# Transposing conv2's outputs: 28 of 64 graphs moved from TensorE to 32x32 blocks on VectorE

## The chip, the cores and the metric

The kernel runs on one core of a Trainium2 chip, in float32 throughout. A core has TensorE (PE in the profile; its weight loads are PEld), VectorE (DVE), ScalarE (ACT), GpSimd (POOL) and SyncE (SP), which work side by side and wait for each other by semaphores. Each takes its own instructions in a fixed order. DMAs are issued from SP, ACT and POOL and share 16 DMA engines. The metric is the device time of one launch in microseconds, as the median of several runs.

## The reference, cut to what matters

There are 64 graphs of 256 nodes with 256 features. Layer 0 is a graph convolution with a residual and a layernorm. Layer 1 takes its output x1 through two branches and a GRU cell:

```
xc     = transpose(x1)                              # features by nodes
h      = relu(bn1(conv1(xc)))                       # kernel size 1
h      = bn2(conv2(h))                              # 17 taps along the nodes
x_conv = transpose(relu(h + xc))
A      = exp(-dist(s, s)) * adj,  s = x1 @ w_se.T + b_se
x_nmp  = A @ relu(x1 @ w_msg.T + b_msg)
r, z, n from x_in = [x_conv, x_nmp] and x1          # GRU cell, weights w_ih, w_hh
out    = layernorm(x1 + (1 - z) * n + z * x1)
```

The change concerns one step: conv2's output plus x1, relu, in the layout that the gate matmuls read.

## The kernel before

**Groups.** The 64 graphs go in four groups of Q = 16. For each graph `layer0` and `layer1` run its two layers up to conv1 and x_nmp. conv2 is computed for a whole group at once by transforms: the group's conv1 outputs are transformed (`p_dft`), multiplied in frequency (`products`, `p_k`), and transformed back on VectorE (`real_transform`, `complex_begin`, `complex_end`). `output` stores the results, nodes by features, to the DRAM tensor `xc_d` of the group (L717). x1 is stored in `x1_d` by layer 0 (L410), and the transposed x1 together with x_nmp in `xn_d` (L509).

**Gates.** `gates(q, part)` runs the GRU cell of graphs of group q. The first EARLY = 4 graphs of groups 0, 1 and 2 run beside the layers of the next group: their pieces are interleaved with `layer0` and `layer1`. Graphs 4 to 15 of those groups run beside the next group's products and inverse transform, at a pace that `paced` sets. The last group has nothing beside it: its 16 gates run alone at the end.

**One gate.** `inputs` is a tile of 128 partitions by 6 by 256: slices 0 and 1 hold x1 transposed, 2 and 3 x_nmp, and 4 and 5 conv2's part (`xcT`). The steps are:

- `load_conv(g)` loads `xc_d` of the graph into the tile `xc_g` (L754, from SP), nodes on the partitions; `load_gate(g)` loads `x1_g` (L758) and slices 0 to 3 of `inputs` (L760).
- `residual(g)` adds x1 to `xc_g` in memory, by an adding DMA issued from POOL (L765).
- `transposed(g)` transposes `xc_g` by four TensorE instructions against the identity into the PSUM bank `p_xcT` (L776). ScalarE reads it, adds the bn2 bias, applies relu and writes `xcT` (L778).
- `input_sums(g)` forms four sums of 128x384 on POOL (L787 to L792, tile `sums`).
- `gru(g)` does seven blocks of three matmuls for r and z (`p_rz`, L808), with the sums as some of the operands, then two times six for n (`p_n`, L845). VectorE adds biases and combines (`first` L821, `trz`, `gn` L850 to L854, L868 to L870), ScalarE does the tanh, and the layernorm's inverse root is a power on POOL (`ln_rs`, L314).

`gru(g)` also prepares its successor: it calls `load_gate(g + 1)`, `residual(g + 1)`, `transposed(g + 1)`, `input_sums(g + 1)` and `load_conv(g + 2)`. `inputs`, `x1_g` and `xc_g` have two buffers each, `sums` one.

**Order.** A scheduler orders each engine's instructions when the kernel is built, by when it expects operands and free buffers; the source's order is a priority, not the outcome. `tc.issue_after(op)` keeps what is written inside it behind `op` on op's engine.

Of the kernel before, what the change touches and what calls it, by code (L numbers as in the profile page):

```python
# [9 lines left out]
F32 = mybir.dt.float32  # L10
AF = mybir.ActivationFunctionType
ALU = mybir.AluOpType
AX = mybir.AxisListType

P = 128
# [11 lines left out]
def kernel(  # L27
# [27 lines left out]
    nc = tc.nc  # L55
    B, N, D = x.shape
# [4 lines left out]
    DCH = D // P  # L61


    FL, NT = 48, 32
    GT = N // NT
    Q = P // GT
    NQ = B // Q
    assert N == 256 and D == 256 and B % Q == 0 and TAPS == FL - NT + 1 and FL == 3 * NT // 2
# [22 lines left out]


    xin, ain = {}, {}

    def load(g):
        if g >= B:
# [51 lines left out]
    bn2_bias = const.tile([P, DCH], F32)  # L148
# [51 lines left out]
    def tables(pool):  # L200
# [24 lines left out]
        with tc.issue_after(DIAGONAL[0]):  # L225
# [6 lines left out]
            for n0, n1 in ((0, 1), (1, 2), (2, 3), (3, 7), (7, NF)):  # L232
                nc.vector.tensor_scalar(
                    w_row[:, :, 1, n0:n1], fwd_row[:, :TAPS, IM[n0] : IM[n0] + n1 - n0], -1.0, None, op0=ALU.mult
                )
        for j in range(GT // 2 + 2):

# [91 lines left out]
    xc_d = [dram.tile([Q, N, D], F32, name=f"xc_d{q}") for q in range(NQ)]  # L329
# [92 lines left out]
    def layer1(g, place):  # L422
# [39 lines left out]

        mid = GT // 2
        if TILES[0] is not V:
# [284 lines left out]

    GATE, CONV, SUMS = {}, {}, {}  # L750

    def load_conv(g):
        CONV[g] = gate.tile([P, NCH, D], F32, name="xc_g")
        nc.sync.dma_start(CONV[g], xc_d[g // Q][g % Q].rearrange("(c p) d -> p c d", p=P))  # L754

    def load_gate(g):
        x1 = gate.tile([P, NCH, D], F32, name="x1_g")
# [2 lines left out]
        nc.sync.dma_start(inputs[:, : 2 * DCH], xn_d[g])  # L760
        GATE[g] = x1, inputs

    def residual(g):

        nc.gpsimd.dma_start(  # L765
            CONV[g], x1_d[g // Q][g % Q].rearrange("(c p) d -> p c d", p=P), accum_op=ALU.add
        )

    def transposed(g):

        xc = CONV.pop(g)
        xcT = GATE[g][1][:, 2 * DCH :]
        p = bank("p_xcT").rearrange("p (k n) -> p k n", k=DCH)
        for k in range(DCH):
            for c in range(NCH):
                nc.tensor.transpose(p[:, k, c * P : (c + 1) * P], xc[:, c, k * P : (k + 1) * P], ident)  # L776
        for k in range(DCH):
            nc.scalar.activation(xcT[:, k], p[:, k], AF.Relu, bias=bn2_bias[:, k : k + 1])  # L778
# [15 lines left out]
    def gru(g):  # L794

        following = g % Q + 1 < Q
        (x1, inputs), S = GATE.pop(g), SUMS.pop(g)
        trz = gate.tile([P, 4, D], F32, name="trz", bufs=1)  # L800
        nn = gate.tile([P, NCH, D], F32, name="nn", bufs=1)
        if following:
            load_gate(g + 1)
        A11, A12, A21, A22 = halves(inputs)

        def block(p, j, a, b):
            for k in range(HALF):
                nc.tensor.matmul(  # L808
                    p[:, j * D : (j + 1) * D], a[:, k], wrz[:, b, k], start=k == 0, stop=k == HALF - 1
                )  # L810

        p15, p26 = accbank("p_rz"), accbank("p_rz")
        block(p15, 0, A11, B11)
        block(p26, 0, A12, B21)
        block(p15, 1, S[:, 0], T1)
        block(p26, 1, S[:, 1], T2)
        yield
        if following:
            residual(g + 1)
        first = gate.tile([P, 2, D], F32, name="first", tag="gn")  # L820
        mark(nc.vector.tensor_add(first, half(p15), brz_t), 1)  # L821
        nc.vector.tensor_add(trz[:, 0:2], first[:, 0:1].to_broadcast([P, 2, D]), half(p26))
        p7, p34 = accbank("p_rz"), accbank("p_rz")
        block(p7, 0, S[:, 2], T3)
        block(p34, 0, S[:, 3], B22)
        block(p34, 1, A22, T4)
        nc.vector.tensor_add(trz[:, 3], trz[:, 1], p7[:, :D])
        mark(nc.vector.tensor_add(trz[:, 1:3], trz[:, 1:4:2], half(p34)), 1)

        nc.scalar.activation(trz[:, 0:4:2], trz[:, 0:4:2], AF.Tanh, scale=0.5)  # L830
        nc.vector.tensor_add(trz[:, 1:4:2], trz[:, 1:4:2], first[:, 1:2].to_broadcast([P, 2, D]))
        nc.scalar.activation(trz[:, 1:4:2], trz[:, 1:4:2], AF.Tanh, scale=0.5)
        if following:
            transposed(g + 1)
        yield
        for c in range(NCH):
            terms = [(inputs[:, k, c * P : (c + 1) * P], wn[:, k]) for k in range(3 * DCH)]
            if c == 0 and following:
                input_sums(g + 1)
            if c == 1 and g % Q + 2 < Q:  # L840
                load_conv(g + 2)
            p = accbank("p_n")
            for o, part in ((1, terms[:DCH]), (0, terms[DCH:])):
                for j, (lhsT, w) in enumerate(part):
                    nc.tensor.matmul(  # L845
                        p[:, o * D : (o + 1) * D], lhsT, w, start=j == 0, stop=j == len(part) - 1
                    )

            gn = gate.tile([P, 2, D], F32, name="gn")
            mark(nc.vector.tensor_add(gn, p.rearrange("p (i d) -> p i d", i=2), bn_t), 1)  # L850
            nc.vector.scalar_tensor_tensor(
                gn[:, 1, :], trz[:, 2 * c], 1.0, gn[:, 1, :], op0=ALU.add, op1=ALU.mult
            )
            nc.vector.scalar_tensor_tensor(  # L854
                gn[:, 0, :], gn[:, 1, :], 0.5, gn[:, 0, :], op0=ALU.mult, op1=ALU.add
            )
            nc.scalar.activation(nn[:, c, :], gn[:, 0, :], AF.Tanh)  # L857


            if g == B - 1:  # L860
                part = slice(c, c + 1)
            elif c == NCH - 1:
                part = slice(0, NCH)
            else:
                yield
                continue
            y, t, n = x1[:, part], trz[:, 1:4:2][:, part], nn[:, part]
            mark(nc.vector.scalar_tensor_tensor(y, t, 3.0, y, op0=ALU.add, op1=ALU.mult), 1)  # L868
            nc.vector.scalar_tensor_tensor(n, t, 1.0, n, op0=ALU.subtract, op1=ALU.mult)
            nc.vector.tensor_sub(y, y, n)  # L870
            layernorm(y, nc.scalar, 4 * LN_EPS)
            nc.scalar.dma_start(out[g].rearrange("(c p) d -> p c d", p=P)[:, part], y)
            yield
# [26 lines left out]
    def run(stage):  # L900
        for _ in stage:
            pass
# [72 lines left out]
        nc.vector.tensor_copy(bn_t[:, 0, :], bih_t[:, 2 * D :])  # L975
        nc.vector.tensor_copy(bn_t[:, 1, :], bhh_t[:, 2 * D :])
    ustream = ctx.enter_context(tc.tile_pool(name="ustream", bufs=6))
    EARLY = 4

    def open_ahead(graphs):  # L980

# [4 lines left out]
    def gates(q, part):  # L986

        for i in part:
            if i == 0:
                load_conv(q * Q)  # L990
                load_gate(q * Q)
                yield
                load_conv(q * Q + 1)
                residual(q * Q)
                yield
                transposed(q * Q)
                yield
                input_sums(q * Q)
                yield
            yield from gru(q * Q + i)  # L1000
# [18 lines left out]
    for q in range(NQ):  # L1019
        first = (q + 1) * Q  # L1020
        more = q + 1 < NQ
        end = chain(complex_end(q), copies(V2) if more else iter(()))
        if more:
            if q:
                others = [take(late, 3 if i % 3 == 0 else 2) for i in range(AHEAD)]
            else:
                others = [nothing() for _ in range(AHEAD)]
                ALONE.update(range(first, first + AHEAD))
            TILES[0] = V2
            begin = graphs(first, range(AHEAD), others)  # L1030
        sums(0)
        real = real_transform()
        for step in range(STEPS):
            if step < 4:
                run(products(step))
            else:
                run(merge(products(step), take(real, 1)))
                run(complex_begin(step))
            if q:
                run(take(late, (0, 1, 1, 1, 1, 1, 2, 1, 2, 1, 2, 1)[step] if more else step % 2))  # L1040
            else:
                run(take(begin, 3))
        run(real)
        if not q:
            run(paced(begin, end, RATES[q]))
        elif more:
            run(paced(chain(merge(take(late, 20), take(begin, 6), 3), begin), end, RATES[q]))
        else:
            run(paced(late, end, RATES[q]))
            run(end)  # L1050
        if more:
            run(late)
            run(end)
            if q == 0:
                scope.close()
                gate = ctx.enter_context(tc.tile_pool(name="gate", bufs=2))
            early = gates(q, range(EARLY))
            others = [take(early, 5 if q == 0 else 2) for _ in range(Q)]
            run(graphs(first, range(AHEAD, Q), others))
            run(early)  # L1060
            if q == 0:
                scope, AHEAD, V2 = open_ahead(6)
                ctx.enter_context(scope)
            late = gates(q, range(EARLY, Q))
        else:
            run(gates(q, range(Q)))


# [51 lines left out]
```

## Time and profile before

| | |
|---|---|
| median of three runs | 2167.7 us (2166.14 to 2169.88) |
| profiled execution | 2162.39 us |
| its span, first to last instruction | 2160.6 us |
| mean granted TensorE clock | 0.993 |
| busy: PE, DVE, ACT, POOL | 2058.4, 1547.2, 834.7, 665.5 us |
| DMA queues of SP, ACT, POOL: share of 16 engines | 30.0%, 8.7%, 8.5% |
| transposes of `xc_g` on PE | 256, four to a graph |
| adding DMAs | 64, issue 1.23 us, 4.8 us to landing (medians) |

All views come from one profiled execution, which is a little shorter than the runs that are timed. A row of a group gives line, engine, operation, the tiles written and read, how many, busy time and mean duration; the idle time before it is named with what ended it. A float32 matmul of 128x256 appears as two records on PE, so "x42" stands for 21 matmuls; a transpose appears as one. A PE duration includes the pipeline's length; back to back, instructions start closer together than they last.

### The profile page before, as it was taken

How to read it: one execution, taken by the hardware profiler on the slowest of the kernel's cores; microseconds unless marked ns; L12 is line 12 of the kernel's file. 1: busy time of each engine (PE TensorE's matmuls, PEld its weight loads, DVE VectorE, ACT ScalarE, POOL GpSimd, SP SyncE). 2: the span in 40 equal slices, each digit the busy share in tenths (PEclk: the TensorE clock that was granted, in tenths of full speed). 3: DMA queues.
4: the chain of work that ended last, by engine and by line, in shares of the span. 5: the costliest groups of instructions: out<-in, count | busy, mean ns of one | idle time of the engine just before them, and what ended most of it. 6: DMA issues, size and time to landing. Idle time of an engine off the chain costs nothing.

```text
span 2160.6 us, 29043 instructions
## 1 busy us (share of the span) xinstructions
PE 2058.4 (95%) x9805; PEld 1745.5 (81%) x9805; DVE 1547.2 (72%) x3691; ACT 834.7 (39%) x1857; POOL 665.5 (31%) x640
## 2 busy tenths in 40 slices
PE   7999999887999999899999999999999998999998
PEld 5888788776788888788888888778888887788887
DVE  5555577775568788775556988876556889977776
ACT  4665643456331123455443122446543122222222
POOL 2444310122431244223222133323231124444442
PEclk9999999999999999999999999999999999999999
DMA  4766666434347644243336654325334834444441
GB/s 122 236 193 199 194 197 209 144 123 153 87 123 228 195 110 135 98 132 113 108 94 189 201 165 112 118 99 153 92 97 134 249 113 120 126 123 103 113 107 54
DMA packets 251182, 305.65 MB, mean 141 GB/s; under 512 B 18174, under 2 KB 229714, under 8 KB 251034
## 3 DMA queue, kind: packets, MB, share of 16 engines
q1 hardware_dynamic: 183530, 200.46, 30.0%
q10 hardware_dynamic: 44480, 67.39, 8.7%
q0 software_dynamic: 23024, 35.95, 8.5%
q8 instruction: 78, 1.28, 0.2%
q14 instruction: 70, 0.57, 0.1%
HBM read 200.62 MB, written 103.06 MB: 141 GB/s over the span
## 4 chain that ended last, share of the span: by engine, by line
PE 45%; DVE 13%; issue 8%; POOL 6%; ACT 4%; DMA 1%; ACTq 0%; POOLq 0%; DVEq 0%
PE p_rz L808 17%; PE p_n L845 8%; PE p_k L530 7%; PE p_out L400 2%; PE p_nmp L504 2%; PE p_hT L390 2%; POOL ln_rs L314 1%; PE p_dft L471 1%; PE p_conv L434 1%; POOL xc_g L765 1%; POOL sums L788 1%; POOL sums L787 1%; PE p_msg L455 1%; PE p_dist L495 1%; ACT inputs L778 1%
## 5 line engine op out<-in xcount | busy, mean ns | idle before, releaser
L845 PE MATMUL p_n<-wn,inputs 128*128 128x256 f32 x1536 | 350.0, 381 | 14.8 <-DVE first L821 14.7
L808 PE MATMUL p_rz<-wrz,sums 128*128 128x256 f32 x1536 | 350.9, 381 | 3.3 <-POOL sums L787 2.4
L845 PEld LDWEIGHTS p_n<-wn,inputs 128*128 128x128 f32 x1536 | 285.8, 190 | 59.7 <-DVE first L821 17.9
L808 PEld LDWEIGHTS p_rz<-wrz,sums 128*128 128x128 f32 x1536 | 290.8, 191 | 48.1 <-issue 5.6
L808 PE MATMUL p_rz<-wrz,inputs 128*128 128x256 f32 x1152 | 271.9, 379 | 0.2
L314 POOL TENSOR_TENSOR ln_rs<-ln_rs,neg_half 128x2 f32<-128x2 f32 x129 | 100.5, 779 | 519.3 <-DVE ln_rs L313 448.0
L808 PEld LDWEIGHTS p_rz<-wrz,inputs 128*128 128x128 f32 x1152 | 217.5, 190 | 30.7 <-issue 1.0
L857 ACT ACTIVATE nn<-gn 128x256 f32<-128x256 f32 x128 | 53.2, 416 | 329.8 <-DVE gn L854 329.5
L530 PE MATMUL p_k<-u,VM 128*128 128x256 f32 x736 | 174.5, 380 | 1.6 <-DVE VM L573 0.9
L787 POOL TENSOR_TENSOR sums<-inputs 128x384 f32<-128x384 f32 x64 | 71.1, 1112 | 332.6 <-ACT inputs L778 299.8
L360 POOL TENSOR_TENSOR dis<-deg,neg_half 128x2 f32<-128x2 f32 x64 | 46.0, 718 | 401.6 <-DVE deg L358 389.6
L324 ACT ACTIVATE x_g<-x_g,ln_mr,ln_rs 128x256 f32<-128x256 f32 x128 | 70.0, 593 | 245.9 <-DVE ln_mr L322 245.9
L530 PEld LDWEIGHTS p_k<-u,VM 128*128 128x128 f32 x736 | 138.3, 190 | 22.5 <-DMA u<-ud 2.0
L471 PE MATMUL p_dft<-fwd,h 128*128 128x240 f32 x512 | 119.8, 378 | 27.8 <-ACT h L438 26.7
L390 PE MATMUL p_hT<-adjT,x 128*128 128x256 f32 x512 | 127.9, 392 | 14.4 <-DVE adjT L372 7.7
L471 PEld LDWEIGHTS p_dft<-fwd,h 128*128 128x128 f32 x512 | 95.4, 192 | 48.4 <-ACT h L438 41.6
L434 PE MATMUL p_conv<-wc,xn 128*128 128x259 f32 x512 | 125.8, 388 | 4.9 <-ACT xn L420 4.9
L383 POOL TENSOR_TENSOR x_t<-x_t,b_t 128x512 f32<-128x512 f32 x64 | 86.5, 1352 | 140.6 <-ACT x L382 88.6
L497 DVE TENSOR_TENSOR aT<-aT,adjT 128x512 f32<-128x512 f32 x64 | 44.3, 692 | 113.5 <-ACT aT L496 113.5
L400 PE MATMUL p_out<-w,hT 128*128 128x256 f32 x512 | 123.1, 383 | 1.4 <-ACT hT L395 0.7
L455 PE MATMUL p_msg<-wmsg,xn 128*128 128x256 f32 x512 | 121.5, 380 | 0.0
L504 PE MATMUL p_nmp<-aT,msg 128*128 128x256 f32 x512 | 121.1, 379 | 0.2 <-DVE aT L497 0.2
(154 smaller groups left out, 3898.6 us busy)
## 6 DMA issues: line engine op xcount, KB each, us to landing
u<-ud SPq DMA_DIRECT2D x284, 256.0 KB
xn_d<-xn ACTq DMA_DIRECT2D x64, 512.0 KB
inputs<-xn_d SPq DMA_DIRECT2D x64, 512.0 KB
ud<-u_set POOLq DMA_DIRECT2D x39, 480.0 KB, 6.0
adj_t<-in_adj_dram SPq DMA_DIRECT2D x64, 256.0 KB
x_t<-in_x_dram SPq DMA_DIRECT2D x64, 256.0 KB
x_d<-x ACTq DMA_DIRECT2D x64, 256.0 KB
xc_d<-VM SPq DMA_DIRECT2D x64, 256.0 KB
```

The lines of the kernel that those rows point to most:

```text
L314: nc.gpsimd.tensor_tensor(rs[:, : len(chunks)], rs[:, : len(chunks)], neg_half[:, : len(chunks)], op=ALU.pow)
L383: nc.gpsimd.tensor_tensor(x_t, x_t, b0_t.unsqueeze(1).to_broadcast([P, NCH, D]), op=ALU.add)
L390: nc.tensor.matmul(p[:, k, :], x1[:, mc, k * P : (k + 1) * P], adjT[:, mc, 1 - mc : 3 - mc, :].rearrange("p n q -> p (n q)"), start=mc == ...
L400: nc.tensor.matmul(p[:, c, :], hT[:, k, c * P : (c + 1) * P], w0[:, k, :], start=k == 0, stop=k == DCH - 1)
L434: nc.tensor.matmul(p, x1T[:, k, c * P : (c + 1) * P], wc1[:, k, :], start=k == 0, stop=k == DCH - 1)
L455: nc.tensor.matmul(p[:, c, :], x1T[:, k, c * P : (c + 1) * P], wmsg[:, k, :], start=k == 0, stop=k == DCH - 1)
L471: nc.tensor.matmul(p[:, t0 * FL : t1 * FL], h[:, c, k * P : (k + 1) * P], fwd[:, first : first + t1 - t0, :].rearrange("p t f -> p (t f)") ...
L504: nc.tensor.matmul(p[:, k, :], msg[:, mc, k * P : (k + 1) * P], aT[:, mc].rearrange("p n q -> p (n q)"), start=mc == 0, stop=mc == NCH - 1,)
L530: nc.tensor.matmul(p[:, j * D : (j + 1) * D], v[:, k, :], u[:, k, :], start=k == 0, stop=k == DCH - 1)
L787: nc.gpsimd.tensor_tensor(S[:, 0], A21, A22, op=ALU.add)
L808: nc.tensor.matmul(p[:, j * D : (j + 1) * D], a[:, k], wrz[:, b, k], start=k == 0, stop=k == HALF - 1)
L845: nc.tensor.matmul(p[:, o * D : (o + 1) * D], lhsT, w, start=j == 0, stop=j == len(part) - 1)
```

## The change

For 28 graphs (the first four of every group, and all of the last group) the transpose goes to VectorE, which transposes each 32x32 block within its 32 partitions. The blocks themselves are put in place by the load: `load_conv` issues four DMAs, one for each 32 features of a 128-feature half, and each moves pieces of 32 floats (128 bytes) so that after the blockwise transpose the tile is the full transpose. x1 is no longer added by the adding DMA. It is added after the transpose by POOL, from the x1 slices of `inputs`, and ScalarE's relu then reads and writes `xcT` in place. `behind` puts the VectorE instructions that are written after a transpose behind it on that engine. The other 36 graphs go as before.

```diff
+    RB = 32
+    NB = P // RB
...
+    order = ExitStack()
+
+    def behind(op):
+        order.close()
+        order.enter_context(tc.issue_after(op.ins))
...
+    EARLY = 4
+
+    def in_blocks(g):
+        return g % Q < EARLY or g >= B - Q
+
     def load_conv(g):
+        y = xc_d[g // Q][g % Q]
+        if in_blocks(g):
+            CONV[g] = gate.tile([P, DCH, N // RB, RB], F32, name="xc_blocks", tag="xc_g")
+            for b in range(NB):
+                nc.sync.dma_start(
+                    CONV[g][b * RB : (b + 1) * RB],
+                    y.rearrange("(s r) (k b j) -> b r k s j", r=RB, k=DCH, j=RB)[b],
+                )
+            return
         CONV[g] = gate.tile([P, NCH, D], F32, name="xc_g")
-        nc.sync.dma_start(CONV[g], xc_d[g // Q][g % Q].rearrange("(c p) d -> p c d", p=P))
+        nc.sync.dma_start(CONV[g], y.rearrange("(c p) d -> p c d", p=P))
...
+    def sent(g):
+        if not in_blocks(g):
+            residual(g)
...
     def transposed(g):
+        inputs = GATE[g][1]
+        xcT = inputs[:, 2 * DCH :]
+        if in_blocks(g):
+            behind(nc.vector.transpose(xcT.rearrange("p k (s r) -> p k s r", r=RB), CONV.pop(g)))
+            nc.gpsimd.tensor_tensor(xcT, xcT, inputs[:, :DCH], op=ALU.add)
+            for k in range(DCH):
+                nc.scalar.activation(xcT[:, k], xcT[:, k], AF.Relu, bias=bn2_bias[:, k : k + 1])
+            return
         xc = CONV.pop(g)
-        xcT = GATE[g][1][:, 2 * DCH :]
...
-            residual(g + 1)
+            sent(g + 1)
...
-                residual(q * Q)
+                sent(q * Q)
```

More of the change, by code (lines that the diff above doesn't have):

```diff
@@ L977 @@
     ustream = ctx.enter_context(tc.tile_pool(name="ustream", bufs=6))
-    EARLY = 4
     def open_ahead(graphs):
@@ L1066 @@
             run(gates(q, range(Q)))
+    order.close()
 _OUT = ((64, 256, 256), "float32")
```

## The prediction

> **What bounds the kernel now.** I read the busy shares first, then the stages, then the chain of waits inside one period, then the tile that the change touches.
>
> ```profile
> PE 2058.4 (95%) x9805; PEld 1745.5 (81%) x9805; DVE 1547.2 (72%) x3691; ACT 834.7 (39%) x1857; POOL 665.5 (31%) x640
> ```
>
> TensorE (PE) is busy for 95% of the span. That is an average, so the next view cuts out three stages: gates beside layers (one period of it), the paced stage (gates of graphs 36 to 47 beside the inverse transform), and the last group's gates. Columns: time, then busy of each engine (instructions), granted clock, DMA share, GB/s.
>
> ```profile
> 1007.00:1047.40 40.40, 39.65 (x196) 33.45 (x194) 22.92 (x62) 19.84 (x47) 11.62 (x12) 1.00 0.34 105
> 1750.00:1900.00 150.00, 137.40 (x641) 118.08 (x640) 142.34 (x297) 34.02 (x71) 59.51 (x53) 1.00 0.43 119
> 1920.00:2137.00 217.00, 217.00 (x1036) 190.79 (x1035) 155.64 (x297) 56.20 (x118) 97.95 (x92) 1.00 0.40 104
> ```
>
> In the last group PE is never idle (217.00 of 217.00) and VectorE (DVE) is busy 72%. Beside layers PE is busy 98% and DVE 57%. Only the paced stage is DVE's (95%), and the change touches none of its graphs. The chain in one period of the last group (start, length, what):
>
> ```profile
> 1931.33 9.06 PE p_rz L808 x42
> 1940.39 0.44 PE p_xcT L776 x4
> 1940.83 5.18 PE p_n L845 x24
> ```
>
> One graph takes 9.06 + 0.44 + 5.18 = 14.68 us, all of it PE, and 0.44 us of that is the four transposes. The tile they read:
>
> ```profile
> L776 PE MATMUL p_xcT<-ident,xc_g x256: 272/273/333, 537.0 to 2131.4; 128*128 128x128 f32 x128
> L765 POOL DMA_DIRECT2D xc_g<-x_d x64: 1183/1230/1692, 529.5 to 2108.5; - x64
>   DMA xc_g<-xc_d: 27.3, 6
> ```
>
> A transpose is recorded with 273 ns, but it occupies PE for 0.44/4 = 0.11 us only: the pitch, not the duration, is what can be saved. The last two lines are GpSimd (POOL): 1.23 us to issue each adding DMA, and six waits before one, 27.3 us, for the load.
>
> **What the Trainium skill says.** (1) "TensorE: Matmul & The Clock Gate", Part 4: a transpose is a matmul against the identity, some 275 ns in a kernel. The trace agrees (273) and shows the pitch of 0.11 us that the page lacks. (2) "VectorE: DVE Perf Modes", The three transpose paths: DVE transposes 32x32 blocks only, so something else has to move the blocks; here the loading DMA does. "Vector Engine (DVE) Microarchitecture Reference", 3.8, gives one element per cycle per lane. That is the rate of a two-input add, and the trace has one of 128x512 at 692 ns; no transpose is in it. (3) "GPSIMD Engine Reference", 3.1: a two-input op is about 2 times slower than on DVE. The trace agrees: 1352 against 692 ns for 128x512. (4) "DMA: Bandwidth & Descriptors", Specifications: line rate needs pieces of 512 B or more. The block loads use 128 B; no run here shows that price.
>
> **The change, part by part** (28 graphs: 0-3, 16-19, 32-35 beside layers, and 48-63).
>
> *Removed from PE.* 28 x 4 transposes at 0.11 us: 28 x 0.44 = **12.3 us**, on the path in both stages.
>
> *Stalls around them.* At the last group's start PE waits 0.44 us for the relu and 0.43 us for the sums of graph 48, at 1917 to 1919. With blocks the relu no longer queues behind PE's 1914.8 transpose: -0.9. At the first group's start PE waits 1.99 us for the sums (541.5 to 543.5): POOL stood in order behind an adding DMA for graph 2, which waited from 537.66 to 540.65 for its load. That DMA is gone and the built order puts graph 0's sums ahead of the next add. Between 0 and -2; I take -1.0.
>
> *POOL.* 28 adding DMAs go (1.23 us each to issue, 34.4 us in all) and 28 adds of 128x512 come (row L383: 1.35 us, 37.8 us). Net +3.4 us on an engine 31% busy, so 0. But the place changes: beside layers the issue stood between the sums and the layernorm's power (1057.92, power at 1058.73, while DVE waited 2.90 us for it, and PE then 0.65 us for h). In the built order the add comes later, just ahead of the next power. 0 to -5; I take -1.0.
>
> *DVE.* 28 transposes, by the nearest row 0.69 us each, 19.3 us. If a 32-bit element took two passes it would be (2 x 512)/512 of the streaming part, about 1.25 us; under 0.69 there is no reason. In the last group DVE has 4.1 us idle of 14.68 per graph, so 0. The place matters: in the built order a transpose stands behind the second p_n addition of graph g and writes the inputs of **g+2**, because that buffer comes free when PE has read it. Its results are wanted one whole period (14.2 us) later. Queued behind it on DVE are the rest of graph g's gate (gn, nn, y, layernorm), whose takers are ScalarE and the output; PE waits for none of it in that period, since its next banks need only `first` and `trz`, due 4 us later than they are ready. Without that cover (were it for g+1) add, relu and sums would come after the PE's second block and cost 2.5 us per graph. Beside layers DVE is also idle 43%, but PE does wait there on short handovers (h, dist_r, msg; 0.2 to 0.65 us). 12 transposes x 0.69 = 8.3 us is the upper bound, 0 the lower; I charge 12 x 0.2 = +2.4.
>
> *DVE slowed by POOL.* The same gn step takes 0.42 us alone and 1.10 us while POOL computes (1945.08 and 1947.36). 28 more POOL ops can stretch 28 DVE ops by 0.7 us; the last group's idle time covers 16. 0 to +8; +1.0 for the other 12.
>
> *ScalarE.* The relu reads SBUF in place of PSUM: 416 ns (row L857) against 468. 0.
>
> *DMA and SP.* One load of 256 pieces of 1 KB becomes four of 512 pieces of 128 B: 84 more issues on SP at 0.37 us. They stand ahead of later x, adjacency and input loads, which are two to three graphs early, and in the last group behind the same graph's inputs. The x1 re-read (256 KB) goes. On the queues: 2048/16 = 128 pieces per engine and graph. q1's mean piece took 30.0% x 16 x 2160.6 / 183530 = 56 ns (1.1 KB), so 7.2 us per graph as an upper estimate if a small piece costs as much as a large one. The load of the block tile for g+2 can start when the previous holder was transposed, two periods ahead: hidden. 0.
>
> Sum: -12.3 -0.9 -1.0 -1.0 +2.4 +1.0 = **-11.8 us**. The profiled execution took 2162.4 us (span 2160.6 and 1.8 around it), so it would take 2150.6. The runs' median, 2167.7, stands 5.3 above it; I apply the difference to that: **2156**.
>
> **Rivals.**
>
> *A: the layer stages give it back.* The last group gains 16 x 0.44 + 0.9 = 7.9, while beside layers the transposes lie on DVE ahead of work that PE waits for: 12 x (0.69 for the transpose + 0.3 of stretching by POOL) = 11.9 against 12 x 0.44 = 5.3 saved. Net 11.9 - 5.3 - 7.9 = -1.3: 2166, no change to be seen. For it: PE's idle time there is all handovers from DVE and ScalarE. Against it: those waits total under 2 us per 40 us, and 2.9 us of DVE's own waiting for POOL lies in the same period.
>
> *B: small pieces bind the DMA queues (slower).* Place: the last group. Of 0.40 x 14.68 = 5.9 us of DMA time per graph some 3 us (the old load at 56 ns, the adding DMA about double) go; 3 stay. The 128 pieces bind from (14.2 - 3)/128 = 88 ns each. At 110 ns a graph takes 3 + 14.1 = 17.1 us, 2.4 more than now, x 15 = +36; less the layers' 5 and the start's 1: +30, **2198**. For it: the skill's 512 B limit. Against: 56 ns is already the mean of pieces eight times as long, so a small one would have to cost 1.6 times a large one.
>
> *C: the cover fails at group starts.* Each of four groups starts with a store of xc_d, then the load. Today load plus adding DMA take some 8 us (529.5 issue, 4.8 to landing). Should four loads of small pieces take 4 us more than that, DVE stands still with the layers' work behind it: 4 x 4 = +16, net +4: 2172.
>
> That the change does nothing is excluded: PE loses 112 instructions in the built program.
>
> **Chances.** Forecast 0.70, A 0.13, B 0.07, C 0.06, others slower 0.04. A measurement of this kernel tells 0.2% (4.3 us) from no change. Faster: 0.70. Within: A, 0.13. Slower: B, C and others, 0.17. The forecast's own range is 2148 to 2163: stalls and the POOL order give up to 7 more, both DVE terms at half their bound 7 less. Reaching to A and the nearest part of C, 2147 to 2169 leaves out B, most of C and a little below.
>
> **What would show it.** In the changed profile: PE at 0.00 for L776 in the last group's period and a period of 14.2 to 14.3 us there; a DVE transpose row of 0.69 (at most 1.25) us, 28 times; POOL adds near 1.35 us; no PE wait on the relu or on the sums inside the last group; 40.4 us periods beside layers down by 0.4 to 1. Wrong if the last group's period stays over 14.6 us with DMA share near 1 (B), if DVE waits for xc_blocks over 3 us at the group starts (C), or if PE's waits for h, msg and dist_r grow (A).

## Result and the profile after

The changed kernel takes 2146.5 us (median of five, 2143.7 to 2154.1) against 2167.7: ratio 0.9903, 95% interval 0.9883 to 0.9924. A second set of runs, with runs of the kernel before between them, gave 0.9915 (0.9903 to 0.9928). The forecast was 2156 with a range of 2147 to 2169: the direction was right, the gain is about 19 to 21 us where 11.7 was forecast, and the time lies just under the range.

Two profiled executions of the changed kernel are used: the first, of 2154.1 us (span 2152.3), and a second, of span 2147.8. The profiled execution of the kernel before lies 5.3 us under its median, the first one after 7.5 over its own, so the spans differ by 8.3 us where the medians differ by 21. Part of that is the granted clock: at 900 to 940 us it is 0.91 in both traces of the changed kernel and 1.00 in the one before, a loss of 2.8 us there; `layers_only` and `dve_add_last`, below, come from the same source up to that point and do not show it.

First trace after, the page: busy time, and the DMA queues of SP (q1) and POOL (q0) with packets, MB and share.

```profile
PE 2052.7 (95%) x9693; PEld 1735.8 (81%) x9693; DVE 1581.6 (73%) x3719; ACT 841.9 (39%) x1857; POOL 664.8 (31%) x640
...
q1 hardware_dynamic: 235050, 200.46, 30.9%
...
q0 software_dynamic: 15408, 28.61, 6.1%
```

The busy shares hardly move, and say little. The new operations, same trace: the tile `xc_blocks`, then the line of the add, each with min/median/max in ns.

```profile
L774 SPq DMA_DIRECT2D xc_blocks<-xc_d x112: 557/624/1817, 526.0 to 2090.5; - x112
L805 DVE STREAM_TRANSPOSE inputs<-xc_blocks x28: 696/701/712, 534.5 to 2115.4; 128x512 f32<-128x512 f32 x28
```

```profile
L806 POOL TENSOR_TENSOR inputs<-inputs x28: 1262/1274/1764, 535.3 to 2117.3; 128x512 f32<-128x512 f32 x28
its engine sat idle before it (us, times) until:
  DMA inputs<-xn_d: 55.3, 15
...
  DMA xc_blocks<-xc_d: 6.5, 1
```

The transpose takes 0.70 us, as forecast; the add takes 1.27 us (1.35 forecast) and waits mostly for the load of `inputs`, not for the blocks. The windows that answer to those shown of before, second trace: one layer period, the paced stage, 15 periods of the last group.

```profile
1004.53:1043.57 39.04, 38.99 (x191) 32.96 (x191) 24.85 (x63) 20.18 (x46) 12.89 (x13) 1.00 0.36 108
1743.40:1893.40 150.00, 140.16 (x641) 120.64 (x640) 142.45 (x297) 34.22 (x72) 58.85 (x52) 0.98 0.43 117
1909.51:2123.18 213.67, 213.67 (x991) 188.10 (x991) 156.24 (x319) 62.19 (x122) 101.65 (x91) 1.00 0.34 92
```

This layer period falls from 40.40 to 39.04 us, by 1.36 where the forecast had 0.4 to 1, and PE's idle time in it from 0.75 to 0.05 us. A period of the last group is 213.67 / 15 = 14.24 us. The chain there, second trace and then first:

```profile
1923.75 9.06 PE p_rz L846 x42
1932.82 5.18 PE p_n L883 x24
1938.00 9.06 PE p_rz L846 x42
```

```profile
1968.16 9.06 PE p_rz L846 x42
1977.23 5.28 PE p_n L883 x24
1982.51 9.06 PE p_rz L846 x42
1991.57 5.42 PE p_n L883 x24
```

The four transposes are gone, and what is left is 9.06 + 5.18. In the first trace `p_n` is stretched to 5.28 and 5.42, because VectorE writes `first` late: from 1925 to 2125 us 13 weight loads of `p_n` wait for it (total, times, longest), and in the second trace none does.

```profile
PEld p_n L883 <- DVE first L859: 4.0, 13, 0.4
```

**Where the time went.** VectorE writes `msg` once per graph and `first` once per gate; these marks can be followed through every trace. Time of a stretch against the trace of before, in us (graphs of `msg`; for the last group `first` of graphs 48 to 63):

| kernel | 28 to 31 | 37 to 47 | 53 to 63 | layers | last group |
|---|---|---|---|---|---|
| changed, first trace | -6.9 | -2.9 | -2.1 | -11.9 | -4.3 |
| changed, second trace | -6.8 | -2.4 | -2.6 | -11.8 | -8.3 |
| layers_only | -7.0 | -2.4 | -2.1 | -11.5 | 0.0 |
| spare_pe | -6.3 | -1.6 | -1.6 | -9.5 | -1.2 |
| spare_issue | -7.0 | -2.7 | -1.8 | -11.5 | -6.0 |
| twice_dve | -6.1 | -0.5 | +0.5 | -6.1 | -2.9 |
| late_relu | -4.8 | +2.1 | +1.9 | -0.8 | -6.1 |
| pe_dve_add | +3.6 | +0.8 | +0.9 | +5.3 | +1.4 |

Of the first column 1.7 us is a stretch at 543 to 548 us in which the trace of before has a granted clock of 0.66. `last_only`, whose first group is as before, has such a dip there too, and no trace of a kernel with blocks beside the layers has it; whether it belongs to the longer wait of PE just ahead of it (1.99 us) is not shown. The table says where time was won, not what the whole execution won: in the second trace the stretches add up to -20.1 us and the span is 12.8 shorter, so 7.3 us are lost between them, 2.8 of these by the clock at 900 to 940.

The columns of the second and third group are sums of a gain and a loss. The three full periods gain 3.6 us, but at the group's start some 1.6 us go: in every kernel with blocks beside the layers, and in none of `before`, `last_only` and `pe_dve_add`. There an operation of VectorE that otherwise takes 0.16 us lasts 1.22, while POOL adds on `x_t`, and PE then waits 1.30 for h (second trace):

```profile
968.25 1.27 POOL L392 TENSOR_TENSOR x_t<-x_t,b_t 128x512 f32<-128x512 f32 x1
```

```profile
968.32 1.22 DVE L331 SCALAR_TENSOR_TENSOR ln_mr<-ln_mv,ln_rs 128x2 f32<-128x2 f32 x1 [0.54 <-POOL ln_rs L323]
```

### The profile page after: what moved, and what is told of

The parts are those of the page before. It is cut to its first block, busy times and chain, and to the rows that moved or that the text cites. A ratio compares the mean times of both kernels' runs of the same rounds, so it can differ in the third digit from the quotient of the medians.

```text
span 2152.3 us, 28977 instructions
## 1 busy us (share of the span) xinstructions
PE 2052.7 (95%) x9693; PEld 1735.8 (81%) x9693; DVE 1581.6 (73%) x3719; ACT 841.9 (39%) x1857; POOL 664.8 (31%) x640
## 3 DMA queue, kind: packets, MB, share of 16 engines
q1 hardware_dynamic: 235050, 200.46, 30.9%
## 4 chain that ended last, share of the span: by engine, by line
PE 44%; DVE 12%; issue 9%; POOL 6%; ACT 4%; DMA 2%; ACTq 0%; SPq 0%; POOLq 0%; DVEq 0%
PE p_rz L846 14%; PE p_n L883 8%; PE p_k L539 7%; PE p_out L409 2%; PE p_nmp L513 2%; PE p_hT L399 2%; PE p_dft L480 2%; POOL ln_rs L323 2%; PE p_conv L443 1%; PE p_msg L464 1%; PE p_dist L504 1%; POOL sums L826 1%; POOL sums L825 1%; DMA u<-ud 1%; POOL xc_g L796 1%
## 5 line engine op out<-in xcount | busy, mean ns | idle before, releaser
L883 PE MATMUL p_n<-wn,inputs 128*128 128x256 f32 x1536 | 355.1, 385 | 13.4 <-DVE first L859 13.2
L480 PEld LDWEIGHTS p_dft<-fwd,h 128*128 128x128 f32 x512 | 95.2, 192 | 47.6 <-ACT h L447 41.2
```

Of the source, the lines that this page charges most:

```text
L480: nc.tensor.matmul(p[:, t0 * FL : t1 * FL], h[:, c, k * P : (k + 1) * P], fwd[:, first : first + t1 - t0, :].rearrange("p t f -> p (t f)") ...
L883: nc.tensor.matmul(p[:, o * D : (o + 1) * D], lhsT, w, start=j == 0, stop=j == len(part) - 1)
```

## The experiments

Theory P says that TensorE's pitch is what is saved. Theory Q says that it is the adding DMA and its issue on GpSimd; it was then split into I (the issue itself) and S (the relu and the sums come earlier). Each was timed in turn with the kernel before.

| kernel | median us | ratio to before | 95% interval |
|---|---|---|---|
| again (the changed kernel) | 2146.2 | 0.9915 | 0.9903 to 0.9928 |
| last_only | 2158.5 | 0.9965 | 0.9952 to 0.9978 |
| layers_only | 2153.6 | 0.9943 | 0.9931 to 0.9955 |
| spare_pe | 2154.0 | 0.9951 | 0.9935 to 0.9967 |
| spare_issue | 2149.7 | 0.9922 | 0.9910 to 0.9934 |
| pe_dve_add | 2171.1 | 1.0022 | 1.0014 to 1.0030 |
| twice_dve | 2157.8 | 0.9953 | 0.9940 to 0.9966 |
| dve_add_last | 2145.7 | 0.9899 | 0.9884 to 0.9914 |
| late_relu | 2157.6 | 0.9962 | 0.9948 to 0.9976 |
| but_paced | 2158.4 | 0.9963 | 0.9950 to 0.9977 |
| all_blocks | 2167.0 | 1.0007 | 0.9999 to 1.0015 |
| no_behind | 2148.9 | 0.9921 | 0.9908 to 0.9933 |

**again.** The kernel unchanged.

> The changed kernel once more, to give its ratio a second interval and a second trace. Both theories: 2143 to 2149 us by the timed runs (first time 2146.5). The first trace had stretches of lower granted clock (0.94 at 900 to 960 us, 0.98 at 1420 to 1520) in which some 4.5 us were lost; if that was chance, a second trace has them elsewhere or not at all, and the layer periods still stand at 39.1 us against 40.4.

The time came as expected. The lower clock at 900 to 940 was there again, so "chance" is not shown for it, and `layers_only` and `dve_add_last` speak against the program alone as its cause. What sets it stays open.

**The two halves.**

```diff
-        return g % Q < EARLY or g >= B - Q
+        return g >= B - Q                      # last_only
+        return g % Q < EARLY and g < B - Q     # layers_only
```

> Blocks for graphs 48 to 63 only. Theory P (TensorE's 0.44 us per graph is what is saved, in both stages): 16 x 0.44 and 0.9 at the group's start, 7.9 us, so 2160. Theory Q (the gain is the adding DMA and its issue on GpSimd gone from the layer stages; the last group has become VectorE's and gains little): 0 to 3 us, so 2165 to 2168.

> Blocks for graphs 0-3, 16-19 and 32-35 only. Theory P by the pitch alone: 12 x 0.44 = 5.3 us and 1 to 2 at the first group's start, 2160 to 2161. Theory Q: the layer periods fall by 1.3 us each, as the first trace shows (40.4 to 39.1), of which 0.44 is the pitch: 12 x 1.1 to 1.3, 13 to 16 us, so 2152 to 2155.

By medians against 2165.1 the last group is worth 6.6 us and the layers 11.5; together 18.0, and the whole change 18.9. So P is right for the last group. In the layers the pitch alone (5.3) cannot pay; there Q, or something else on that chain, has to.

**spare_pe.**

```diff
+            spare = bank("p_xcT").rearrange("p (k n) -> p k n", k=DCH)
+            for k in range(DCH):
+                for c in range(NCH):
+                    nc.tensor.transpose(spare[:, k, c * P : (c + 1) * P], ident, ident)
             behind(nc.vector.transpose(xcT.rearrange("p k (s r) -> p k s r", r=RB), CONV.pop(g)))
```

> The changed kernel with four transposes of the identity put back on TensorE for each of the 28 graphs, into a bank that nobody reads; all else as changed. It gives the removed pitch back and nothing else. Theory P: 28 x 0.44 = 12.3 us slower than the changed kernel, 2159. Theory Q with VectorE binding the last group at 14.3 us a graph: 12 x 0.44 beside layers and 16 x 0 to 0.3 in the last group, 5 to 10 us slower, 2152 to 2157.

It is 7.8 us slower by medians. In the last group its period is 14.68 us again, exactly as before: there the pitch is the whole gain of a period. Beside the layers it gives back 2.3 of 11.8 us (table of stretches), not 5.3. So 9.5 us, or 7.8 without the clock at 543 us, come without any pitch saved.

**spare_issue and pe_dve_add.** The first puts an issue on POOL back; the second keeps PE's transposes, takes the adding DMA of the 28 graphs away and lets VectorE add x1 in its place.

```diff
+        if in_blocks(g) and g < B - Q:                       # spare_issue, behind the last sum
+            with tc.issue_after(last.ins):
+                nc.gpsimd.dma_start(spare_d[g], x1_d[g // Q][g % Q])
```

```diff
-            behind(nc.vector.transpose(...))                 # pe_dve_add
-            nc.gpsimd.tensor_tensor(xcT, xcT, inputs[:, :DCH], op=ALU.add)
+            for k in range(DCH):
+                for c in range(NCH):
+                    nc.tensor.transpose(p[:, k, c * P : (c + 1) * P], xc[:, c, k * P : (k + 1) * P], ident)
+            behind(nc.vector.tensor_add(xcT, p, inputs[:, :DCH]))
```

> The changed kernel with a DMA of 256 KB issued by GpSimd right behind the four input sums of graphs 0-3, 16-19 and 32-35, from the x1 array into a DRAM array that nobody reads: the issue alone is back where it stood, without its wait for the load. Theory I (the layer periods got shorter because that issue, 1.2 us, no longer stands ahead of the layernorm's power): 12 x 0.6 to 0.9 us slower than the changed kernel, 2152 to 2157. Theory S (they got shorter because the sums themselves come earlier, no longer waiting in the same period for PE's transposes and the relu): the issue falls where nobody waits, 0 to 2 us slower, 2146 to 2149.

> For the same 28 graphs the transposes stay on TensorE from a plain load, and VectorE adds x1 (already transposed in the inputs) to the bank; the adding DMA is gone, and so is the add on GpSimd. It removes what the change removes from DMA and GpSimd, and nothing of TensorE's. Theory I: the layer stages keep 8 to 10 us of their gain, the last group gains nothing: 2155 to 2158 where the kernel before has 2165. Theory S: transposes, add, relu and sums stand in one chain in the same period as before, so only the first group's start gains: 2163 to 2166, and GpSimd's sums begin 3 to 4 us after the transposes in the layer periods, as before.

Once the sums are early, the issue costs next to nothing. (The spare issue took 0.59 us and ended 0.4 us before the power had its operand; one of 1.24 us, like the adding DMA's, would have delayed the power by some 0.25.) That does not yet refute I for the kernel before, where the sums are late.

`pe_dve_add` is 5 us slower than the kernel before, worse than either theory had it, and does not decide between them. First, a loss that belongs to neither: +3.6 us lie in the first group. There POOL ran six operations in a row from 581.6 to 588.0 us, an operation of VectorE that otherwise takes 0.42 us lasted 6.32, and PE waited 5.35 for h. Second, the issue is still there. The adding DMAs of a group are issued in the order of its graphs, and in the kernel before the one at 1057.92 is the fifth of its group: that of graph 20, which is not among the 28. In `pe_dve_add` it and the next one stand behind the sums in two of the three layer periods of a group, and in the first period none does. The first period, POOL and then PE, and the second:

```profile
1024.56 0.70 POOL L323 TENSOR_TENSOR ln_rs<-ln_rs,neg_half 128x2 f32<-128x2 f32 x1
```

```profile
1028.48 1.89 PE L480 MATMUL p_dft<-fwd,h 128*128 128x240 f32 x8 [0.25 <-ACT h L447]
```

```profile
1064.26 1.20 POOL L796 DMA_DIRECT2D xc_g<-x_d  x1
1065.05 1.15 POOL L323 TENSOR_TENSOR ln_rs<-ln_rs,neg_half 128x2 f32<-128x2 f32 x1
```

```profile
1069.35 1.89 PE L480 MATMUL p_dft<-fwd,h 128*128 128x240 f32 x8 [1.42 <-ACT h L447]
```

Up to the power POOL does the same in both, with the sums late. With the issue the power ends 1.2 us later, PE waits 1.42 us for h in place of 0.25, and the period is 41.2 us in place of 39.7 (40.4 in the kernel before); groups 1 and 2 show the same. So the issue does cost time where the sums are late, as I says.

**late_relu.** A test of S: everything as changed, but nine relus wait for something late.

```diff
+            if shifted(g + 1):     # in_blocks, before the last group, not a group's first
+                bias = small.tile([P, DCH], F32, name="late_bias", bufs=2)
+                nc.vector.scalar_tensor_tensor(
+                    bias, trz[:, 1, 0:DCH], 0.0, bn2_bias[:, 0:DCH], op0=ALU.mult, op1=ALU.add
+                )
+                LATE[g + 1] = bias
             transposed(g + 1)
```

> The changed kernel, but the relu of graphs 1-3, 17-19 and 33-35 takes its bias from a 128x2 tile that VectorE writes after the gate of the graph before has had its last addition to trz (one operation of 128x2 more per graph): the blocks, the transposes, the adds and the DMA are as changed, only relu and input sums come late again, as they did behind PE's transposes. Theory S (the layer periods got shorter because sums and the layernorm's power on GpSimd come earlier): power ends 2 us later again, PE waits 0.6 us for h and 0.2 us for dist_r in each of nine graphs, 5 to 8 us slower than the changed kernel, 2151 to 2154. If the gain came from elsewhere, only the small operations count, 9 x 0.2: 2146 to 2148.

It is 11.4 us slower by medians, and the layer stretches lose 11.0 of their 11.8 us (table), more than expected. A late relu alone, with no issue ahead of the power, thus brings the wait back; the small operations that make it late take 0.15 us each. The 11.0 us are not the measure of S, though: the relu comes later here than in the kernel before. POOL in one layer period, kernel before, changed kernel (second trace) and `late_relu`; columns: start, length, line, operation, and in brackets the idle time before it with what ended it:

```profile
1050.30 0.71 POOL L360 TENSOR_TENSOR dis<-deg,neg_half 128x2 f32<-128x2 f32 x1 [8.85 <-DVE deg L358]
1053.54 1.00 POOL L787 TENSOR_TENSOR sums<-inputs 128x384 f32<-128x384 f32 x1 [2.53 <-ACT inputs L778]
...
1056.98 1.00 POOL L792 TENSOR_TENSOR sums<-inputs,sums 128x384 f32<-128x384 f32 x1
1057.92 1.24 POOL L765 DMA_DIRECT2D xc_g<-x_d  x1
1058.73 1.18 POOL L314 TENSOR_TENSOR ln_rs<-ln_rs,neg_half 128x2 f32<-128x2 f32 x1
```

```profile
1046.38 0.71 POOL L369 TENSOR_TENSOR dis<-deg,neg_half 128x2 f32<-128x2 f32 x1 [7.96 <-DVE deg L367]
1047.06 1.00 POOL L825 TENSOR_TENSOR sums<-inputs 128x384 f32<-128x384 f32 x1
...
1050.51 1.00 POOL L830 TENSOR_TENSOR sums<-inputs,sums 128x384 f32<-128x384 f32 x1
1052.43 0.71 POOL L323 TENSOR_TENSOR ln_rs<-ln_rs,neg_half 128x2 f32<-128x2 f32 x1 [0.93 <-DVE ln_rs L322]
```

```profile
1050.65 1.50 POOL L831 TENSOR_TENSOR sums<-inputs 128x384 f32<-128x384 f32 x1 [4.01 <-ACT inputs L814]
...
1054.13 1.00 POOL L836 TENSOR_TENSOR sums<-inputs,sums 128x384 f32<-128x384 f32 x1
1055.09 0.71 POOL L323 TENSOR_TENSOR ln_rs<-ln_rs,neg_half 128x2 f32<-128x2 f32 x1
```

Before, the sums waited 2.53 us for the relu, which waited for PE's transposes of the same period; the layernorm's power stood behind them and ended 9.6 us after `dis` began. Two links of that chain can be read off: the wait of 2.53 us, and the issue behind the sums, with which the power ends 1.9 us after them, where it needs 0.7. In the changed kernel the operand is ready a period ahead, the sums start at once behind `dis`, the issue has moved to another place (1031.9 us), and the power waits for VectorE instead: it ends 6.8 us after. In `late_relu` the sums start 4.7 us after `dis` began (3.2 before) and the power ends 9.9 after. Its taker is VectorE, then h, then PE's `p_dft`. PE at `p_dft` in that period, in the same order:

```profile
1063.07 1.89 PE L471 MATMUL p_dft<-fwd,h 128*128 128x240 f32 x8 [0.65 <-ACT h L438]
```

```profile
1058.09 1.89 PE L480 MATMUL p_dft<-fwd,h 128*128 128x240 f32 x8
```

```profile
1058.95 1.89 PE L480 MATMUL p_dft<-fwd,h 128*128 128x240 f32 x8 [1.34 <-ACT h L447]
```

The wait of 0.65 is gone in the changed kernel and is 1.34 in `late_relu`: 0.7 more than before, of which 0.44 is PE being there earlier by the transposes that it no longer does. Three layer periods (1510.7 to 1632.0 us before) take 121.25 us before, 117.63 in the changed kernel's second trace, 118.22 in `spare_pe` and 122.10 in `late_relu`. PE's start times split the gain of 3.6 into 1.3 of pitch and 2.3 of waits for h and what follows from it, at `p_dft`, `p_hT` and `p_dist`. `spare_pe` keeps 3.0 of it: the early power is worth that much by itself, the pitch 0.6 on top.

What is shown, then: beside the layers the gain hangs on when the power ends. A late relu and an issue behind the sums each delay it, and the change took both from there at once. How they share the gain is not measured. Either delay (2.5 and 1.2 us) is longer than PE's wait of 0.65, so by this estimate removing one of them might have been enough.

**twice_dve.**

```diff
+            y = CONV.pop(g)
+            nc.vector.transpose(xcT.rearrange("p k (s r) -> p k s r", r=RB), y)
-            behind(nc.vector.transpose(xcT.rearrange("p k (s r) -> p k s r", r=RB), CONV.pop(g)))
+            behind(nc.vector.transpose(xcT.rearrange("p k (s r) -> p k s r", r=RB), y))
```

> The changed kernel with each of the 28 block transposes done twice on VectorE (the same result written again). The forecast charged 0.2 us for one beside layers and nothing in the last group: 12 x 0.2, 2.4 us slower, 2148 to 2150. Rival: VectorE's loop is what binds in both stages: 12 x 0.7 and 16 x 0.3 to 0.7, 13 to 19 us slower, 2159 to 2165.

Slower by 11.6 us, nearer to the rival. The stretches give 5.7 us beside the layers, 0.48 per transpose, and 5.3 in the last group, 0.33 each (against the second trace). A second transpose is free in neither stage; what the first one costs was not isolated.

**dve_add_last.**

```diff
+            adder = nc.vector if g >= B - Q else nc.gpsimd
+            adder.tensor_tensor(xcT, xcT, inputs[:, :DCH], op=ALU.add)
```

> The changed kernel with x1 added by VectorE in the last group (16 graphs), by GpSimd beside layers as changed. The two traces of the changed kernel have a last group of 14.24 us periods in one and of 14.26 to 14.48 in the other, where VectorE's operations are stretched while GpSimd computes. Theory M (the stretching by GpSimd's add is what makes the slow one): every period 14.24, 2143 to 2146, 1 to 3 us under the changed kernel. Rival: VectorE's own load decides, and 0.7 us more per graph makes the slow one permanent: 2149 to 2153.

Its trace has 14.24 us in every period, but so have the second trace of the changed kernel and those of `spare_issue`, `late_relu` and `all_blocks`, and its interval overlaps both of the changed kernel's. So the times do not decide. What the traces do show is how the two executions of the changed kernel differ. VectorE and then POOL, first trace (periods of 14.24 to 14.56):

```profile
1957.06 0.70 DVE L805 STREAM_TRANSPOSE inputs<-xc_blocks 128x512 f32<-128x512 f32 x1
...
1959.00 1.49 DVE L907 SCALAR_TENSOR_TENSOR nn<-trz,nn 128x512 f32<-128x512 f32 x1 [0.48 <-ACT nn L895]
```

```profile
1958.68 1.27 POOL L806 TENSOR_TENSOR inputs<-inputs 128x512 f32<-128x512 f32 x1 [4.21 <-DVE gn L892]
```

And the second trace (14.24):

```profile
1955.98 0.69 DVE L907 SCALAR_TENSOR_TENSOR nn<-trz,nn 128x512 f32<-128x512 f32 x1 [0.48 <-ACT nn L895]
```

```profile
1956.81 1.72 POOL L806 TENSOR_TENSOR inputs<-inputs 128x512 f32<-128x512 f32 x1 [5.37 <-DVE nn L907]
```

Where the add starts ahead of L907, L907 takes 1.4 to 1.7 us instead of 0.69 (11 of 14 periods in the first trace); where it starts after, L907 keeps its 0.69 (all 14 in the second). VectorE was busy 108.71 of 129.65 us in the nine periods of the first trace from 1925.09, 84%, against 73% above. But the stretching does not suffice for the longer periods: `spare_issue` has it in 11 of 14 too, and PE keeps 14.24 in all of them. What else it takes is open.

**More graphs, and no rule of order.**

```diff
+        return g < 36 or g >= B - Q            # but_paced
+        return True                            # all_blocks
```

```diff
-            behind(nc.vector.transpose(...))                 # no_behind
+            nc.vector.transpose(...)
```

> Blocks for 52 of 64 graphs: all but 36 to 47, whose stage is VectorE's (95% busy). If what was gained per graph beside layers also holds beside the inverse transforms (graphs 4-15 and 20-31, where PE is busy 95 to 97%): 24 x 0.2 to 0.44, 5 to 10 us faster than the changed kernel, 2136 to 2141. Rival: a further transpose on VectorE costs there what it costs beside layers when done twice (0.48 us), as much as PE saves: 2144 to 2148.

> Blocks for all 64 graphs. As the kernel before it, and 12 more transposes of 0.70 us in the stage that VectorE binds (graphs 36 to 47): 12 x 0.7 to 1.0, 8 to 12 us slower than with 52 graphs. If that stage has room after all: no slower.

> The changed kernel without the rule that keeps what is emitted after a block transpose behind it. In the built program TensorE's order is the same and VectorE's differs by a few small operations of the adjacency (deg, adeg) that move by a place or two: within 2 us of the changed kernel, 2144 to 2148. If the rule keeps transposes out of the way of the layers: 3 to 8 us slower.

Blocks for 24 more graphs cost 12 us, worse than either theory had it, and 12 more cost another 9; all 64 together are no faster than none. PE's waits in `but_paced` between 640 and 900 us:

```profile
PE p_dist L504 <- DVE dist_r L497: 4.4, 2, 3.7
PE p_n L883 <- DVE first L859: 4.2, 2, 2.7
```

Both are for VectorE, which is busy 216 of these 260 us in the changed kernel and 228 in `but_paced`; the changed kernel has 1.8 and 1.4 us of these waits. Dropping `behind` costs nothing that these runs can tell. No kernel tried is measurably faster than the changed one.

## Why the prediction was right and where it was wrong

- **PE's pitch, -12.3.** Right in the last group: 14.68 to 14.24 us, with `spare_pe` giving exactly 14.68 back. Beside the layers `spare_pe` gives back only 2.3 of 5.3 us.
- **POOL's order, -1.0 of 0 to -5.** This is the step that failed: the term was sized far too small. The prediction saw the wait (2.90 us of VectorE for the power, 0.65 of PE for h), put it down to the issue alone, and took a fifth of the bound. The six full periods of groups 1 and 2 alone gave 2 x 2.3 = 4.6 us of waits, and with PE's transposes put back the layers still gain 9.5 us, 7.8 without the clock (`spare_pe`). The link that the prediction left out is the relu, and with it the sums, behind PE's transposes of the same period; it had seen that the inputs become ready a period ahead and used that only as cover for VectorE. The issue that it names is a real link (`pe_dve_add`), but the one that it shows, at 1057.92, belongs to graph 20, which keeps its adding DMA: it moved away and did not disappear. With the relu late (`late_relu`) the layers gain only 0.8 us, although PE's transposes are gone: saved pitch is of no use while that wait stands.
- **Stall at the first group's start, -1.0.** PE's wait for the sums went from 1.99 to 0.43 us, but the one for the relu from 0.14 to 0.97: -0.7. **At the last group's start, -0.9:** the two waits of graph 48 are gone, as forecast. In the second trace PE waits 1.31 for `first` just ahead of them (0.27 before), so that nothing is left; in the first trace it waits 0.36.
- **VectorE, +2.4 and +1.0.** The duration (0.69 forecast, 0.70) was right. A second transpose costs 0.48 beside layers, so 0.2 was too low for a further one; what the first costs by itself was not isolated. Stretching by POOL did come, 1.6 us at each of two group starts, but by POOL's addition on `x_t`, not by the new adds. In the last group "0" held in the second trace and not in the first, where `first` comes late and half of the gain is lost (-4.3 against -8.3).
- **Layers together:** forecast -5.3 -1.0 -1.0 +2.4 +1.0 = -3.9, measured -11.5. **Last group:** forecast -7.9, measured -6.6. The miss lies in the layers.
- **ScalarE, DMA, SP at 0.** The relu from SBUF takes 0.51 us (416 ns assumed), without effect. A block load's issue takes 0.62 us, not 0.37, and stays hidden.
- **Rival A** fails as a whole: the layers gain more than the last group, though the waits that it names do grow at the two group starts. **Rival B** fails by far: SP's queue time rose by 30.9% x 16 x 2152.3 - 30.0% x 16 x 2160.6 = 270 us of engine time, plus 28 x 256 large pieces at 56 ns that went, 671 us over 57,344 small pieces: 12 ns each, where 88 would bind. **Rival C:** POOL waits 6.5 us once for the blocks, VectorE not at all; the losses at the group starts have another cause (above).

## What to carry to other kernels

When an operation is moved off the bounding engine, look past its pitch at the chain that stood behind it: here an operand became ready a period earlier and a DMA issue moved away, and an in-order helper engine (POOL) reached an unrelated short operation 2.8 us sooner. A wait that the profile shows at the bounding engine should be priced by following every link of its chain back, not by the last instruction queued in front of it. A move that pays in stages where the receiving engine has room (57 and 72% busy) can cost where it has less (24 more graphs cost 12 us, where VectorE was busy 83%): price the second unit, not only the first. And look in the trace of an experiment whether what it takes away is really gone from the place in question: in `pe_dve_add` another graph's issue stood there.

## What the runs showed of the hardware

- VectorE's 32x32 transpose of 128x512 float32 takes 0.70 us, like a two-input addition (0.69); pieces of 128 bytes cost about 12 ns of one DMA engine each, one fifth of the 56 ns of 1.1 KB pieces.
- Removing 28 adding DMAs took 8.5% x 16 x 2160.6 - 6.1% x 16 x 2152.3 = 837 us of engine time off POOL's queue, 30 us each.
- VectorE's operations of 0.69 us take 1.3 to 1.8 us when an operation of POOL on 128x512 has started just ahead of them, and keep their 0.69 when they start first; then the add of 1.27 us is the one that lasts longer, up to 1.8 (first and second trace, `spare_issue`). Behind six operations of POOL in a row one of 0.42 us took 6.32 (`pe_dve_add`).
- Short dips of the granted clock (0.66 over 5 us, 0.91 over 40; inside them it is 0.50, as from 908.4 to 915.2 us in the second trace) cost 1.7 and 2.8 us at places that differ between traces of one program: differences of 2 us between two traces should be placed before they are explained.
